# Layer 0's attention heads packed into dense tiles of eight for the output projection, and the projection moved within the order of steps

## The chip, the cores and the metric

The kernel runs on one NeuronCore of a Trainium2 chip. A core has five engines that run side by side: TensorE (PE in the profile; its weight loads are PEld), VectorE (DVE), ScalarE (ACT), GpSimd (POOL) and SyncE (SP, which here only issues transfers). They work on a common on-chip memory, SBUF, of 128 partitions; TensorE writes to a second one, PSUM, whose banks hold 512 float32 values per partition. The metric is the device time of one execution in microseconds (us). A comparison uses the median of several executions.

## The reference, cut to what matters

The model has four layers, each of a cross attention and a feed-forward part, over x of shape (4, 256, 256), four batches of 256 tokens of width 256, with a context of shape (4, 512, 128). All is float32. Only the attention of layer 0 and the step from it to layer 0's feed-forward part are touched:

```python
x = x + _L0_xattn_ref(_layernorm(x), ctx_1024, ...)
x = x + _L0_ffn_ref(_layernorm(x), ...)

def _L0_xattn_ref(x, y, Wq, bq, Wk, bk, Wv, bv, Wkv_dca, bkv_dca, ...):
    # H = 16 heads of HD = 16, DCA = 16
    y_dca, y_main = y[:, -16:, :], y[:, :-16, :]
    kv_dca = (y_dca @ Wkv_dca + bkv_dca).reshape(b, 16, 2, H, HD)
    k_dca, v_dca = _ln(kv_dca[:, :, 0], ...), kv_dca[:, :, 1]
    q = _ln((x @ Wq + bq).reshape(b, s1, H, HD), ...)
    kv = concatenate([y_main @ Wk + bk, y_main @ Wv + bv], -1).reshape(b, s2, H, 2 * HD)
    k, v = _ln(kv[..., :HD], ...), kv[..., HD:]
    ctx = _attn(q, k, v) + _attn(q, k_dca, v_dca)      # both per head, softmax(q k / 4) v
    return ctx @ Wo + bo                               # (256 -> 256)

def _L0_ffn_ref(x, A, B, W, bias):
    vecs = einsum('arh,bsh->bsar', A, x)               # 64 arrows of rank 16
    routes = the four arrows of largest norm, a quarter each
    v = einsum('bsa,bsar->bsr', routes, vecs)
    return x @ W.T + bias + einsum('bsa,ajr,bsr->bsj', routes, B, v)
```

There are thus two softmaxes per head, one over 496 context rows and one over the last 16, and their results are added before the output projection.

## The kernel before

Layer 0's attention (in `bounded_path`, lines 1026 to 1611) stands under a manual schedule: each engine runs its instructions in the order in which the program writes them. What is written first is queued first, and an instruction that waits holds up all behind it on its engine.

The attention loops over the four batches b and, in each, over four groups hg of four heads, each in two steps kp of two context tiles of 128: eight steps i = 2 * hg + kp per batch. A step writes, in this order: `scores` (16 short matmuls into four PSUM banks and four Exp on ScalarE, into pT); `ahead(b, i)` (work for the next batch: the query and key scaling's last product at i = 5, the transposes into qT and kT at 6 and 7); `values` of the group before (matmuls into po) and, where kp is 1, its `quotient`; then `between(b, i)`, the rest of the next batch's preparation (projections at i = 1 to 3, `project_v` among them, the Ln and Exp of the scaling at 4, batch norm statistics at 5 and 6) and `output0` of the batch before. The quotient of a batch's last group is written at i = 1 of the next batch.

Each head has 32 partitions of po: 16 of ones in the values, which give the softmax's denominator, and 16 of the values proper. po has two halves of 256 tokens, for the two softmaxes. `quotient` turns 32x32 blocks of po on VectorE, takes the reciprocal of row 0 of each block, turns it back as a broadcast, multiplies po with it (o), and GpSimd adds the two halves into oT[:, hg]. Half of oT's partitions hold quotients of the ones. `output0` multiplies, per chunk of 128 tokens, the four groups of oT with wo0 (py), whose rows for those partitions are zero (padded on the host); VectorE adds the bias (y_sb) and GpSimd adds that to x_sb. `bias_rows`, `bias_columns` and `output_bias` carry the values' biases through wo0 into bo0.

PSUM banks are handed out by `bank`: while layer 0 runs, all tags but "o" share one ring of six banks in program order, so that a tile waits for the release of the tile six before it; "o" has two of its own. The tag y_sb has two SBUF buffers, shared by output0 and the feed-forward part.

In batch 3 the same places hold layer 0's feed-forward preparation: layer norms (names with f), the `Arrows` of chunk 0 at i = 6 (`vectors`: the matmuls paf and copies into two) and 7 (`routes`: VectorE finds the four largest norms and weighs; GpSimd's last product goes into the second half of two). After the loop (lines 1603 to 1611) come the last values and quotient, the vectors of chunks 1 and 2, the routes of chunk 1, and `output0(B - 1)`; then the pool l0 is closed, and a loop over the eight chunks n runs `routes` of n + 2, `turned` (transposes of two into puT, copied into uT), `vectors` of n + 3 and `output` (pyf, ys, x_sb), with the folding of layer 1's weights between. Those weights' loads (line 969) reuse l0's memory and wait for its last readers.

The call sites of the change, cut:

```python
            if b > 0 and i in (4, 5):
                output0(b - 1, (i - 4,))
...
        for n in (1, 2):
            arrows[n] = Arrows(n)
            arrows[n].vectors()
        arrows[1].routes()
        output0(B - 1)
        c0.close()
```

Of the kernel before, what the change touches and what calls it, by code (L numbers as in the profile page):

```python
# [17 lines left out]
P = 128  # L18
# [817 lines left out]
def bounded_path(ctx: ExitStack, tc: tile.TileContext, t, out: bass.AP, over):  # L836
# [189 lines left out]
    with tc.manual_schedule(engines={E.PE, E.Activation, E.DVE, E.Pool}):  # L1026
# [39 lines left out]
            load_c(b)  # L1066
            load_x(b)

        wo0 = l0.tile([P, 4, D], F32, tag="wo0", name="wo0")
        nc.sync.dma_start(wo0, t["L0_wo"].rearrange("(g p) n -> p g n", p=P))  # L1070
        bo0 = bcast(l0, t["L0_bo"], D, "bo0")
        wa = load_fw("wa", [P, ND, NA * RA], lambda w: [(w, t["F0_aT"].rearrange("(d p) n -> p d n", p=P))], "wa", f0w)
        wb = load_fw("wb", [P, 8, D], lambda w: [(w, t["F0_bT"].rearrange("(k p) n -> p k n", p=P))], "wb", f0w)
# [28 lines left out]

        vals = [l0.tile([P, NK, H0, 32], F32, tag=f"vals{i}", name=f"vals{i}") for i in range(2)]
        vals_d = [l0.tile([P, H0, 32], F32, tag=f"vals_d{i}", name=f"vals_d{i}") for i in range(2)]

        def ones_of_values():
            nc.gpsimd.memset(rows, 1.0)
            nc.gpsimd.affine_select(  # L1110
                out=rows[:, 0:1], in_=rows[:, 0:1], compare_op=ALU.is_ge, fill=0.0, base=RD - 1,
                pattern=[[0, 1]], channel_multiplier=-1,
            )
            nc.gpsimd.affine_select(
                out=rows[:, 1:2], in_=rows[:, 1:2], compare_op=ALU.is_ge, fill=0.0, base=-RD,
                pattern=[[0, 1]], channel_multiplier=1,
            )
            for i in range(2):
                nc.gpsimd.memset(vals[i][:, : NK - 1, :, :HD0], 1.0)
                nc.gpsimd.tensor_copy(  # L1120
                    vals[i][:, NK - 1, :, :HD0], rows[:, 0:1, None].to_broadcast([P, H0, HD0])
                )
                nc.gpsimd.tensor_copy(vals_d[i][:, :, :HD0], rows[:, 1:2, None].to_broadcast([P, H0, HD0]))


        def head_sums(src, p=P):
# [57 lines left out]

        def project_v(b):

            wv = by_head(wkv, 2 * HD0)[:, :, :, HD0:]
            for k0 in range(0, NK + 1, 2):
                pv = bank("mm", [P, 2, H0, HD0], f"pv{b}_{k0}")
                for k in range(k0, min(k0 + 2, NK + 1)):  # L1190
                    ck = c_last[:, b % 2, k - NK + 1, :] if k >= NK - 1 else cT[:, b, k * P : (k + 1) * P]
                    nc.tensor.matmul(pv[:, k - k0], lhsT=ck, rhs=wv[:, int(k == NK)], start=True, stop=True)
                if k0 < NK:
                    nc.scalar.copy(vals[b % 2][:, k0 : k0 + 2, :, HD0:], pv)
                else:
                    nc.scalar.copy(vals_d[b % 2][:, :, HD0:], pv[:, 0])

        class Scale:

# [61 lines left out]
            nc.vector.tensor_tensor(within, wmx[:, 0:1], wmx[:, 1:2], ALU.mult)  # L1261
            nc.vector.tensor_scalar(within, within, SMAX * SMAX * 4.0, None, ALU.is_le)

        bcol = l0.tile([P, 4, P], F32, tag="bcol", name="bcol")

        def bias_rows():

            nc.vector.tensor_tensor(brow[:, 0, :], brow[:, 0, :], brow[:, 1, :], ALU.add)

        def bias_columns():  # L1270
            pc = bank("o", [P, 4], "pbrow")
            for g in range(4):
                nc.tensor.matmul(
                    pc[:, g : g + 1], lhsT=brow[:, 0, g * P : (g + 1) * P], rhs=ident[:1, :1], start=True, stop=True
                )
            nc.vector.tensor_copy(bcol, pc[:, :, None].to_broadcast([P, 4, P]))

        def output_bias():
            pb = bank("mm", [P, D], "pbo")
            for g in range(4):  # L1280
                nc.tensor.matmul(pb, lhsT=bcol[:, g, :], rhs=wo0[:, g, :], start=(g == 0), stop=(g == 3))
            nc.vector.tensor_tensor(bo0, bo0, pb, ALU.add)

        kTs, qTs = {}, {}
# [42 lines left out]
        def values(b, hg, pT, po, ks, dca):  # L1327

            for k in ks:
                for j in range(4):  # L1330
                    nc.tensor.matmul(  # L1331
                        po[32 * j : 32 * (j + 1), 0, :],
                        lhsT=vals[b % 2][:, k, 4 * hg + j, :],
                        rhs=pT[k // 2][:, j, k % 2, :],
                        start=(k == 0),
                        stop=(k == NK - 1),
                    )
            if dca:
                for j in range(4):
                    nc.tensor.matmul(  # L1340
                        po[32 * j : 32 * (j + 1), 1, :],
                        lhsT=vals_d[b % 2][:, 4 * hg + j, :],
                        rhs=pT[1][:, j, 1, :],
                        start=True,
                        stop=True,
                    )

        def quotient(b, hg, po, oT):

            NB0 = 2 * S // 32  # L1350
            po = po.rearrange("p a s -> p (a s)")
            z = w0.tile([P, NB0, 32], F32, tag="z0", name=f"z0_{b}_{hg}")
            z_f = z.rearrange("p f i -> p (f i)")
            nc.vector.transpose(z_f, po)
            rz = small.tile([P, NB0], F32, tag="rz0", name=f"rz0_{b}_{hg}")
            nc.vector.reciprocal(rz, z[:, :, 0])
            nc.vector.transpose(z, rz[:, :, None].to_broadcast([P, NB0, 32]))
            o = w0.tile([P, 2, S], F32, tag="o0", name=f"o0_{b}_{hg}")
            nc.vector.tensor_tensor(o.rearrange("p a s -> p (a s)"), po, z_f, ALU.mult)
            nc.gpsimd.tensor_tensor(oT[:, hg, :], o[:, 0], o[:, 1], ALU.add)  # L1360

        def output0(b, chunks=range(NC)):
            for c in chunks:
                py = bank("mm", [P, D], f"py0_{b}_{c}")
                for hg in range(4):
                    nc.tensor.matmul(
                        py,
                        lhsT=oTs[b][:, hg, c * P : (c + 1) * P],
                        rhs=wo0[:, hg, :],
                        start=(hg == 0),  # L1370
                        stop=(hg == 3),
                    )
                y_sb = w0.tile([P, D], F32, tag="y_sb", name=f"y_sb{b}_{c}")
                nc.vector.tensor_tensor(y_sb, py, bo0, ALU.add)
                nc.gpsimd.tensor_tensor(x_sb[b][:, c, :], x_sb[b][:, c, :], y_sb, ALU.add)
# [83 lines left out]
        xn = norm.tokens()  # L1459
        warm(8)  # L1460
        xnTs[0] = layernorm_T(xn, "a0_0")
        centred(by_head(wq0), by_head(wq0), mq)
        centred(by_head(crow), by_head(crow), head_sums(by_head(crow), 3), 3)
        wk = by_head(wkv, 2 * HD0)[:, :, :, :HD0]
# [48 lines left out]
        def between(b, i):  # L1513

            n = b + 1
            if n < B:
# [21 lines left out]
                    norms[n + 1] = Norm(n + 1, f"a0_{n + 1}")  # L1538
                elif i == 6 and n + 1 < B:
                    xns[n + 1] = norms[n + 1].tokens()  # L1540
            if b > 0 and i in (4, 5):
                output0(b - 1, (i - 4,))
            if b == 0:
                if i == 0:
                    bias_rows()
# [38 lines left out]

        before = None
        for b in range(B):
            oTs[b] = w0.tile([P, 4, S], F32, tag="oT0", name=f"oT0_{b}")
            for hg in range(4):
                pT = [
                    w0.tile([P, 4, 2, S], F32, tag="pT0", name=f"pT0_{b}_{hg}_{kp}", bufs=3) for kp in range(2)  # L1590
                ]
                for kp in range(2):
                    scores(b, hg, pT, kp)
                    ahead(b, 2 * hg + kp)
                    if before:
                        if kp == 0:
                            po = bank("o", [P, 2, S], f"po0_{b}_{hg}")
                        values(*before, po, (2 * kp, 2 * kp + 1), kp == 1)
                        if kp == 1:
                            quotient(*before[:2], po, oTs[before[0]])  # L1600
                    between(b, 2 * hg + kp)
                before = (b, hg, pT)
# [3 lines left out]
        for n in (1, 2):  # L1606
            arrows[n] = Arrows(n)
            arrows[n].vectors()
        arrows[1].routes()
        output0(B - 1)  # L1610
        c0.close()

# [13 lines left out]
        for n in range(B * NC):  # L1626
            if n + 2 < B * NC and n != 5:
                arrows[n + 2].routes()
            if c2s:
                b, c2 = c2s.pop()  # L1630
                nc.vector.tensor_reduce(csq[:, b * NK : (b + 1) * NK], c2, AX.X, ALU.add)
            arrows[n].turned()
            if n % NC == 0:
                if n + 3 < B * NC:
                    arrows[n + 3] = Arrows(n + 3)
                    arrows[n + 3].vectors()
                for _ in range((0, 0, 1, 1, 2, 2, 1, 1)[n]):
                    next(fold)
                arrows[n].output()
            else:  # L1640
                arrows[n].output()
                k = n // NC + 2
                if k < B:
                    xnTs["f", k] = layernorm_T(xns["f", k + (k == 2)], f"f0_{k}")
                for _ in range((0, 0, 1, 1, 2, 2, 1, 1)[n]):
                    next(fold)
                if n == 5:
                    arrows[7].routes()
                if n + 3 < B * NC:
                    arrows[n + 3] = Arrows(n + 3)  # L1650
                    arrows[n + 3].vectors()
# [1545 lines left out]
```

## Time and profile before

| | us |
|---|---|
| median of 3 runs (lowest to highest) | 1463.46 (1458.37 to 1465.62) |
| the profiled execution's own time | 1460.66 |
| its span, first to last instruction | 1458.9 |
| mean granted TensorE clock | 0.992 |
| TensorE busy in the span | 1422.8 |
| layer 0's attention, first scores to last py | 25.1 to 172 |

The profile shows one execution. Busy time of TensorE is the time in which a matmul is in flight; the duration of a row of the profile is from issue to end and contains the pipeline's latency, so that the price of a matmul in a stream is better read from the distance of two starts. A wait is put down to the releaser that came last by the profile. The chain that ended last follows the work back from the last instruction and tells which engine's instruction set the pace at each time.

### The profile page before, as it was taken

To read this page: it belongs to the slowest core of one execution; us is meant where nothing else is said; L and a number is where in the kernel's file an instruction comes from. 1 tells how busy PE (TensorE), PEld (TensorE's weight loads), DVE (VectorE), ACT (ScalarE), POOL (GpSimd) and SP (SyncE) were. 2 spreads that over 40 slices of the span, in tenths; PEclk is the share of its full clock that TensorE was granted. 3 is DMA by queue.
4 is the path that set the end of the run, shared out by engine and by line. 5 is a ranking of instruction groups with operands and counts; after the bars stand their busy time and mean duration, and the time that the engine had idled before them with its cause. 6 is when DMAs were issued, how large, how long until landed. Compare 5 with 4: busy or idle time off the path is not lost.

```text
span 1458.9 us, 20220 instructions
## 1 busy us (share of the span) xinstructions
PE 1422.8 (98%) x7421; PEld 937.1 (64%) x7421; DVE 912.8 (63%) x2004; ACT 585.9 (40%) x1124; POOL 678.8 (47%) x796
## 2 busy tenths in 40 slices
PE   8999999999999999999999999999999999999997
PEld 7666567565566666877555666656875566666656
DVE  5666783566766557543577566557755766767675
ACT  4666443433433332244543333333454433333331
POOL 3122232486545455132356665655313765456560
PEclk9999999999999999999999999999999999999999
DMA  5000111310000000264120000000241000000000
GB/s 166 2 1 2 48 61 37 74 36 0 8 1 8 1 0 9 62 189 119 33 66 8 19 4 1 8 1 8 86 132 44 19 1 1 0 1 0 0 1 32
DMA packets 49591, 47.06 MB, mean 32 GB/s; under 512 B 8169, under 2 KB 45386, under 8 KB 49484
## 3 DMA queue, kind: packets, MB, share of 16 engines
q1 hardware_dynamic: 45884, 37.56, 8.6%
q0 software_dynamic: 2496, 6.82, 1.8%
q8 instruction: 61, 1.00, 0.3%
q10 hardware_dynamic: 1104, 1.31, 0.3%
q14 instruction: 46, 0.38, 0.1%
HBM read 38.86 MB, written 6.82 MB: 31 GB/s over the span
## 4 chain that ended last, share of the span: by engine, by line
PE 88%; DVE 7%; POOL 2%; issue 1%; ACT 1%; DVEq 0%; ACTq 0%; POOLq 0%
PE ps L1818 22%; PE po L1826 21%; PE paq L1788 5%; PE pao L1788 4%; PE pbq L1788 4%; PE pbo L1788 4%; PE pgu L2326 2%; PE ps L1321 2%; PE po L1331 2%; PE pyf L1448 2%; PE paf L1398 1%; PE py L1908 1%; PE pm L985 1%; PE psh L2162 1%; PE pn L1001 1%
## 5 line engine op out<-in xcount | busy, mean ns | idle before, releaser
L1837 POOL TENSOR_TENSOR half<-pT 128x1024 f32<-128x1024 f32 x93 | 218.8, 2353 | 320.7 <-ACT pT L1821 262.4
L1818 PE MATMUL ps<-qT,cT 128*128 128x512 f32 x768 | 345.5, 592 | 0.0
L1826 PE MATMUL po<-pT,c_sb 128*128 128x512 f32 x768 | 345.3, 592 | 0.0
L1821 ACT ACTIVATE pT<-ps,mbias 128x512 f32<-128x512 f32 x384 | 263.7, 687 | 155.5 <-PE ps L1818 142.2
L1826 PEld LDWEIGHTS po<-pT,c_sb 128*128 128x128 f32 x768 | 145.8, 190 | 183.2 <-issue 183.2
L1818 PEld LDWEIGHTS ps<-qT,cT 128*128 128x128 f32 x768 | 138.9, 190 | 138.4 <-issue 137.0
L1830 ACT COPY oT<-po 128x512 f32<-128x512 f32 x96 | 56.2, 586 | 265.0 <-PE po L1826 265.0
L1873 POOL TENSOR_TENSOR oT<-oT,wide 128x512 f32<-128x512 f32 x90 | 115.5, 1302 | 28.1 <-DVE wide L1872 28.1
L1325 ACT ACTIVATE pT<-ps 128x512 f32<-128x512 f32 x128 | 66.1, 603 | 42.0 <-PE ps L1321 41.8
L1798 DVE TENSOR_TENSOR qT<-qT,paq 128x128 f32<-128x128 f32 x90 | 25.4, 282 | 85.9 <-ACT qT L1797 85.8
L1798 DVE TENSOR_TENSOR w<-w,pao 128x128 f32<-128x128 f32 x21 | 6.0, 285 | 109.3 <-ACT w L1797 109.3
L1847 DVE STREAM_TRANSPOSE turned<-half 128x512 f32<-128x512 f32 x96 | 68.3, 711 | 6.3
L1845 DVE TENSOR_TENSOR half<-half 128x512 f32<-128x512 f32 x96 | 70.6, 735 | 2.5 <-POOL half L1837 2.2
L1788 PEld LDWEIGHTS paq<-xnT_a,m_sb 128*128 128x128 f32 x360 | 57.9, 191 | 21.5 <-issue 10.6
L1788 PE MATMUL paq<-xnT_a,m_sb 128*128 128x128 f32 x360 | 71.4, 280 | 0.1
L1788 PE MATMUL paq<-xx,m_x 128*128 128x128 f32 x360 | 69.8, 275 | 0.0
L1851 DVE TENSOR_REDUCE sums<-turned 128x16 f32<-128x512 f32 x96 | 65.8, 686 | 3.3
L1788 PE MATMUL pao<-n_x,ox 128*128 128x128 f32 x336 | 65.2, 276 | 0.3 <-POOL ox L1714 0.3
L1872 DVE STREAM_TRANSPOSE wide<-rz 128x512 f32<-128x512 f32 x96 | 62.2, 685 | 0.1
L1797 ACT COPY qT<-paq 128x128 f32<-128x128 f32 x90 | 23.9, 265 | 88.7 <-PE paq L1788 88.7
L1801 DVE TENSOR_TENSOR qT<-qT,pbq 128x384 f32<-128x384 f32 x90 | 49.8, 554 | 9.4
L1788 PEld LDWEIGHTS paq<-xx,m_x 128*128 128x128 f32 x360 | 54.7, 192 | 0.0
(445 smaller groups left out, 2614.6 us busy)
## 6 DMA issues: line engine op xcount, KB each, us to landing
wo<-in_L_wo SPq DMA_DIRECT2D x12, 512.0 KB
wq<-in_L_wqT SPq DMA_DIRECT2D x11, 512.0 KB
yd<-yr SPq DMA_DIRECT2D x23, 128.0 KB
w<-in_F_w SPq DMA_DIRECT2D x4, 512.0 KB
xd<-xn_f SPq DMA_DIRECT2D x7, 256.0 KB
wk<-in_L_wkT SPq DMA_DIRECT2D x11, 128.0 KB
wv<-in_L_wvT SPq DMA_DIRECT2D x11, 128.0 KB
x_sb<-in_x SPq DMA_DIRECT2D x4, 256.0 KB
```

The lines of the kernel that those rows point to most:

```text
L1325: nc.scalar.activation(pT[kp][:, j], ps[j], AF.Exp)
L1788: nc.tensor.matmul(p[:, at, :], lhsT=lhsT, rhs=rhs, start=(k == 0 and at == 0), stop=(k == len(of) - 1 and i == which[-1]),)
L1818: nc.tensor.matmul(ps, lhsT=cT[:, b, k * P : (k + 1) * P], rhs=qT, start=True, stop=True)
L1821: nc.scalar.activation(pT[:, k, :], ps, AF.Exp, bias=mbias[:, b, k : k + 1])
L1826: nc.tensor.matmul(po, lhsT=c_sb[:, b, k, :], rhs=pT[:, k], start=(k == 0), stop=(k == NK - 1))
L1830: done["head"] = nc.scalar.copy(raw, po).ins
L1837: nc.gpsimd.tensor_tensor(half, pT[:, 0:2], pT[:, 2:4], ALU.add)
L1845: nc.vector.tensor_tensor(part, half[:, 0], half[:, 1], ALU.add)
L1847: nc.vector.transpose(turned.rearrange("p f i -> p (f i)"), part)
L1851: nc.vector.tensor_reduce(sums[b, hp // 4][:, hp % 4, :], turned, AX.X, ALU.add)
L1872: nc.vector.transpose(wide, rzs[b, hp // 4][:, hp % 4, :, None].to_broadcast([P, NB, 32]))
L1873: eng.tensor_tensor(outs[b, hp], outs[b, hp], wide.rearrange("p f i -> p (f i)"), ALU.mult)
```

## The change

The values of four heads and their ones are stored in two ways: for even groups hg the ones stand in the first 16 of a head's 32 partitions, for odd groups in the last 16. The reciprocal is turned back with zeros for the ones' partitions (rz0, two tiles set to zero once, of which every quotient writes one column), so that the product o is zero there. An even group and the odd one after it are then added into one tile of oT of eight heads: two halves for the even group (one GpSimd addition), and two more for the odd one (two additions). oT and wo0 have two tiles instead of four, output0 two matmuls per chunk instead of four, and the bias functions are cut alike. wo0 is loaded by eight transfers of 16 partitions, which pick its rows. The value weights are first copied by GpSimd into wvo, in the order of the new tiles, and project_v evicts each bank in two copies. ones_of_values follows.

In the order of work, output0 of the batch before goes from steps 4 and 5 to steps 6 and 7, except in batch 3, and after the loop `turned` and `output` of chunk 0 stand before output0 of batch 3 instead of in the loop over n.

```diff
-        wo0 = l0.tile([P, 4, D], F32, tag="wo0", name="wo0")
-        nc.sync.dma_start(wo0, t["L0_wo"].rearrange("(g p) n -> p g n", p=P))
+        wo0 = l0.tile([P, 2, D], F32, tag="wo0", name="wo0")
+        wo0r = t["L0_wo"].rearrange("(q o j i x) n -> o j i x q n", q=2, o=2, j=4, i=2)
+        for o in range(2):
+            for j in range(4):
+                r0 = 32 * j + HD0 * (1 - o)
+                nc.sync.dma_start(wo0[r0 : r0 + HD0], wo0r[o, j, 1])
...
+        halves = [(slice(HD0, 32), slice(0, HD0)), (slice(0, HD0), slice(HD0, 32))]
+        rz0 = [l0.tile([P, 2 * S // 32, 2], F32, tag=f"rzh{i}", name=f"rzh{i}") for i in range(2)]
+        wvo = l0.tile([P, 2, 2, H0 // 2, HD0], F32, tag="wvo", name="wvo")
...
                 for k in range(k0, min(k0 + 2, NK + 1)):
...
-                    nc.tensor.matmul(pv[:, k - k0], lhsT=ck, rhs=wv[:, int(k == NK)], start=True, stop=True)
-                if k0 < NK:
-                    nc.scalar.copy(vals[b % 2][:, k0 : k0 + 2, :, HD0:], pv)
-                else:
-                    nc.scalar.copy(vals_d[b % 2][:, :, HD0:], pv[:, 0])
+                    nc.tensor.matmul(pv[:, k - k0], lhsT=ck, rhs=wvo[:, int(k == NK)], start=True, stop=True)
+                for o, (h, _) in enumerate(halves):
+                    if k0 < NK:
+                        nc.scalar.copy(vals[b % 2][:, k0 : k0 + 2, o, :, h], pv[:, :, o])
+                    else:
+                        nc.scalar.copy(vals_d[b % 2][:, o, :, h], pv[:, 0, o])
...
         def output_bias():
             pb = bank("mm", [P, D], "pbo")
-            for g in range(4):
-                nc.tensor.matmul(pb, lhsT=bcol[:, g, :], rhs=wo0[:, g, :], start=(g == 0), stop=(g == 3))
+            for g in range(2):
+                nc.tensor.matmul(pb, lhsT=bcol[:, g, :], rhs=wo0[:, g, :], start=(g == 0), stop=(g == 1))
...
             nc.vector.transpose(z_f, po)
-            rz = small.tile([P, NB0], F32, tag="rz0", name=f"rz0_{b}_{hg}")
-            nc.vector.reciprocal(rz, z[:, :, 0])
-            nc.vector.transpose(z, rz[:, :, None].to_broadcast([P, NB0, 32]))
+            odd = hg % 2
+            rz = rz0[odd]
+            nc.vector.reciprocal(rz[:, :, 1 - odd], z[:, :, HD0 * odd])
+            nc.vector.transpose(
+                z.rearrange("p f (i x) -> p f i x", i=2), rz[:, :, :, None].to_broadcast([P, NB0, 2, HD0])
+            )
             o = w0.tile([P, 2, S], F32, tag="o0", name=f"o0_{b}_{hg}")
             nc.vector.tensor_tensor(o.rearrange("p a s -> p (a s)"), po, z_f, ALU.mult)
-            nc.gpsimd.tensor_tensor(oT[:, hg, :], o[:, 0], o[:, 1], ALU.add)
+            oT = oT[:, hg // 2, :]
+            nc.gpsimd.tensor_tensor(oT, oT if odd else o[:, 1], o[:, 0], ALU.add)
+            if odd:
+                nc.gpsimd.tensor_tensor(oT, oT, o[:, 1], ALU.add)
 
         def output0(b, chunks=range(NC)):
             for c in chunks:
                 py = bank("mm", [P, D], f"py0_{b}_{c}")
-                for hg in range(4):
+                for q in range(2):
                     nc.tensor.matmul(
                         py,
-                        lhsT=oTs[b][:, hg, c * P : (c + 1) * P],
-                        rhs=wo0[:, hg, :],
...
+                        lhsT=oTs[b][:, q, c * P : (c + 1) * P],
+                        rhs=wo0[:, q, :],
...
         xnTs[0] = layernorm_T(xn, "a0_0")
+        for n in range(2):
+            wv = by_head(wkv, 2 * HD0)[:, n, :, HD0:].rearrange("p (q o j) x -> p o q j x", q=2, o=2)
+            for o in range(2):
+                nc.gpsimd.tensor_copy(wvo[:, n, o].rearrange("p (q j) x -> p q j x", q=2), wv[:, o])
...
-            if b > 0 and i in (4, 5):
-                output0(b - 1, (i - 4,))
+
+            i0 = 4 if b == B - 1 else 6
+            if b > 0 and i in (i0, i0 + 1):
+                output0(b - 1, (i - i0,))
...
         arrows[1].routes()
+        arrows[0].turned()
+        arrows[0].output()
         output0(B - 1)
         c0.close()
...
-            arrows[n].turned()
+            if n:
+                arrows[n].turned()
             if n % NC == 0:
...
-                arrows[n].output()
+                if n:
+                    arrows[n].output()
```

## The prediction

> **What bounds the kernel.** I read the page first, then the rows of the lines that the edit touches, then the chain that ended last between 58 and 182 us, and last the timeline around each wait in it.
>
> ```profile
> span 1458.9 us, 20220 instructions
> PE 1422.8 (98%) x7421; PEld 937.1 (64%) x7421; DVE 912.8 (63%) x2004; ACT 585.9 (40%) x1124; POOL 678.8 (47%) x796
> PE 88%; DVE 7%; POOL 2%; issue 1%; ACT 1%; DVEq 0%; ACTq 0%; POOLq 0%
> ```
>
> TensorE is the bound: a matmul taken away counts in full, unless TensorE then meets a wait. Layer 0's attention runs from about 25 to 172 us.
>
> ```profile
> L1366 PE MATMUL py<-wo,oT x64: 379/379/483, 78.4 to 171.8; 128*128 128x256 f32 x64
> L1360 POOL TENSOR_TENSOR oT<-o x16: 722/728/825, 46.0 to 169.0; 128x256 f32<-128x256 f32 x16
> ```
>
> Each float32 matmul stands as two records, so output0's 32 matmuls are 64, eight per chunk. The 379 ns are latency; the price is the pitch, in the chain (start, duration in us, what):
>
> ```profile
> 78.49 1.94 PE py L1366 x8
> 80.45 0.42 DVE y_sb L1374
> ...
> 82.12 1.76 DVE pad L1231
> ...
> 87.55 0.34 DVE y_sb L1374
> 87.93 1.09 PE pT L1296 x8
> ...
> 120.89 0.34 DVE y_sb L1374
> 121.28 1.09 PE pT L1296 x8
> ...
> 134.82 1.06 DVE xn_f L925 x2
> ...
> 169.01 0.73 POOL oT L1360
> 169.79 2.43 PE py L1366 x10
> ```
>
> A chunk costs 1.94 us. In batches 1 and 2 the chain leaves TensorE between 80 and 88 and at 120: step 6's transposes take a PSUM bank of the ring of six that step 5's py holds until VectorE, behind pad and a quotient, has added the bias. The timeline (start, duration, instruction, in brackets the idle time before and its releaser) gives the waits:
>
> ```profile
> 87.93 0.85 PEld L1296 LDWEIGHTS pT<-ident,pad 128*128 128x128 f32 x8 [1.66 <-DVE y_sb L1374]
> 134.90 0.82 POOL L1360 TENSOR_TENSOR oT<-o 128x256 f32<-128x256 f32 x1 [2.87 <-DVE o L1359]
> 166.69 1.93 POOL L1427 TENSOR_TENSOR twof<-routef,vf 128x1024 f32<-128x1024 f32 x1 [5.65 <-DVE vf L1426]
> 169.78 2.02 PEld L1366 LDWEIGHTS py<-wo,oT 128*128 128x128 f32 x10 [1.99 <-POOL oT L1360]
> ```
>
> **The change part by part, for the profiled execution** (1460.66 us, span 1458.9; 1.8 us lie outside the span, and the shown runs' median is 2.8 us higher, so I take the difference to the median).
>
> *Start.* project_v's evictions go from three to six on ScalarE. Rows: 128x512 copies 585 ns, 128x256 378 ns, and a 128x128 copy elsewhere (L1797) 265 ns. Back to back the three start at 16.81, about 17.3 and 17.75 and make way at 18.02, 1.21 us; four at about 0.28 and two at about 0.17 are 1.46. Behind them wait the Ln of the query scale (18.02), its pad, and TensorE's transposes (20.13), with 0.06 us to spare: **+0.2**. For batches 1 to 3 ScalarE idles 0.28 to 0.69 us around these copies. wvo's four POOL copies fit between 7.67, where POOL goes idle, and 14.05, where project_v starts: a 128x112 copy is 0.28 to 0.57 us, and one copy blocked by VectorE took 0.89, so 1.2 to 3.6 us. Uncovered they would cost that. ones_of_values grows by some 0.7 us of POOL near 22; its consumers start at 37.4. The eight wo0 issues on SP at about 0.45 us push bo0, wa, wb, ww, bias0 and the mask 3.2 us back; first use of wo0 is at 45.4, of the mask 61.8, of wa 151: nothing.
>
> *Bias.* bias_columns loses 4 of 8 records; seven took 0.87 us at 35.55, on TensorE's path: **-0.45**. output_bias loses half of its 1.94 us, but TensorE then waits anyway: from 43.43 the chain is on VectorE without a gap (z, hv, he, pad) until the transposes at 52.04. **0**; it would be -0.97 if that chain were shorter.
>
> *Batch 1, steps 4 to 7.* Scores of step 5 start at 78.5, not 80.43. hr comes off ScalarE at 80.11 as before, since it stands behind step 4's Exps. VectorE's he need no longer wait behind y_sb (80.45), and its second product takes 0.26 us, not the 0.72 it took beside POOL's x_sb addition: pad ends at 82.76, not 83.88. TensorE is there at 82.2, waits 0.65, transposes (1.46), values 1.00, py at half price 0.97: step 7 at 86.3, not 90.02. Now the ring: with py inside step 6, step 7's fourth score bank is that of the second transpose, which VectorE evicts only after pad, the quotient and the batch norm statistics (82.76 + 2.5 + 1.37 + 0.81), 87.5. Scores end at 88.2, not 91.1. Transposes wait 0.1 for y_sb; transposes, values and the rest 2.9, py 0.97: the next batch starts at 92.2, not 93.99. **-1.8.**
>
> *Batch 2.* The same count: pad at 117.4, transposes until 118.9, values, py, step 7 at 120.9 (the bank is free at 120.7, there being no next norm), next batch 125.84, not 127.36. **-1.5.** The waits removed here and in batch 1 are partly replaced by those for pad and the bank.
>
> *Batch 3.* Its two chunks stay in steps 4 and 5, 0.97 us less each: **-1.94**. Odd quotients put a second addition of 0.73 us on POOL, eight in all. Behind it stand oT's reader (late steps, over 10 us away) and VectorE operations that POOL blocks. The row: xn_f at 134.74 takes 820 ns beside POOL's addition, 404 alone, and TensorE waits for it at 135.26 and 135.93. This quotient is odd, so a second addition follows directly: 0 to 0.75, **+0.35** taken, half-way, because the blocked VectorE operation may get in between the two. The rule that speaks against the change is in the Trainium skill (GPSIMD Engine Reference, Specifications): POOL's SBUF interfaces are shared with VectorE and contend with its two-port modes and with two SBUF inputs. Were all eight additions to block the path, the rule gives 8 x 0.73 = 5.8 us, an estimate. The rows limit it: after the other odd quotients follow y_sb or qk (PSUM and one SBUF input; L1168 beside a POOL addition takes its usual 0.68), statistics or nothing.
>
> *End.* Before: paf until 166.74, six py records, wait until 169.79, ten more, turned, paf of chunk 3, output until 180.84. After: turned(0) waits for POOL's twof at 168.62, so the wait of about 2 us stays and only changes its cause. Then turned 0.87, output 0.86 + 3.45 (uT is copied during the first), py 8 records at 0.213 = 1.7, paf 3.44: 179.02. oT, now two additions after twof, is ready at 170.5 and needed at 173.9. **-1.8.** What is late next: the second y_sb shares two buffers with ys, freed by POOL only behind twof of chunk 1 (176.4) and its own addition, at 177.1; VectorE's routes(2) starts 2.7 us later. Their product was ready at 182.8 and is read at 190.25 by TensorE, now 1.8 earlier: 2.9 us remain. The raw loads behind c0.close waited for y_sb (175.09), are needed at 194.99, and move by under 2 us. At 232 to 241 TensorE waits again on VectorE, whose chain there starts from TensorE's own pn, so the gain passes through.
>
> Sum: 0.2 - 0.45 - 1.8 - 1.5 - 1.94 + 0.35 - 1.8 = **-6.95 us**; 1463.46 - 7 = **1456.5**.
>
> **Rivals.** (a) *Larger gain*: the bank wait in step 7 (1.0 with y_sb's) doesn't come, and batch 3's cold stretch goes. The clock row:
>
> ```profile
> 138.00:140.00 2.00, 2.00 (x24) 0.77 (x20) 0.07 (x1) 1.59 (x4) 0.00 (x0) 0.50 0.00 0
> ```
>
> (the last three columns are granted clock, DMA share and GB/s.) Half clock from 137.8 to 141.8 cost 0.58 + 0.42 + 0.62 = 1.6 us. Then -7 - 1.0 - 1.6 = -9.6, 1453.9. For it: a cold stretch hangs on where TensorE's idle time falls, and every start shifts. Against: the xn_f wait stays. (b) *Part is absorbed*: the routing chain on VectorE at 160 to 176 is as long as TensorE's work; if VectorE's 2.7 us are not covered and the start loses more, 4 us go: -3, 1460.5. For it: TensorE waits there already. Against: 2.9 us of slack. (c) *Slower*: new half-clock stretches. They cost 1.6 us at 138 and 0.94 + 1.69 = 2.6 at 30 to 35, 2.1 on average. From four of them (new waits in steps 6 and 7 of batches 1 and 2, and the end) the gain is gone: -7 + 4 x 2.1 = +1.4, 1464.9. The Trainium skill (TensorE: Matmul & The Clock Gate, Part 1) has the clock fall after an idle window of some 3.4 us; by that rule waits of 0.65 to 2 us cost nothing and (c) is nil. The trace is harsher: 1.2 and 0.2 us of idle inside 134 to 136 were enough. But waits of 1.4 at 86.5 and 1.6 at 168.2 left the clock at 1.00, so a stretch per wait is the exception, and four are unlikely. (d) *The moves do nothing*: the halved records alone give 8 x 0.97 + 0.45 - 0.55 = -7.7, 1455.8; nearly the same time, told apart by the waits alone.
>
> **How the numbers follow.** Forecast with (d) 0.55, own range 1454.5 to 1458.5 (half a us for each of four estimated terms); (a) 0.25; (b) 0.15; (c) 0.05. The runs before spread by 0.5%, 7.3 us, which is about what a measurement can tell from no change. The range 1451 to 1461.5 takes in (a) and (b) with the runs' scatter and leaves (c) out. Faster by over 0.5%, below 1456.1: (a) and a bit under half of the forecast, 0.50. Slower by over 0.5%: less than half of (c), 0.02. Within: 0.48.
>
> **What would show it.** py has 32 records, each chunk 0.97 us in the chain. The wait for y_sb at step 6 is gone; in its place waits for pad of under 1 us and, in batch 1 alone, for the fourth bank. xn_f's wait in batch 3 is up to 0.75 longer. turned(0) waits about 2 us for twof, and no py waits for oT. Half clock shows twice, near 30 and 135. The stages after 250 us keep their lengths. I am wrong if the end's waits grow beyond 2.5 us, if project_v's first matmul waits for wvo, or if a third cold stretch shows.

## The result, and the profile after

The changed kernel takes 1454.80 us (median; 1452.88 to 1461.86), the kernel before, run beside it, 1463.19 us (1458.16 to 1469.85). The ratio of the compared runs is 0.9962, with a 95% interval of 0.9948 to 0.9976: 5.6 us less, where 7 were forecast. The runs of both kernels scatter over some 10 us, because TensorE's clock falls in the first 50 us of some executions and not of others (two traces of the changed kernel below differ by 6.8 us in span, 6.5 of them there); so the medians differ by 8.4 us, and the ratio, with its interval, is what I go by.

The head of the changed kernel's page, and the two rows that answer to those shown of before:

```profile
span 1459.7 us, 20196 instructions
PE 1423.3 (98%) x7381; PEld 936.3 (64%) x7381; DVE 913.0 (63%) x2005; ACT 586.2 (40%) x1136; POOL 686.1 (47%) x816
PE 88%; DVE 6%; POOL 2%; issue 1%; ACT 1%; DVEq 0%; ACTq 0%; POOLq 0%
...
L1392 PE MATMUL py<-wo,oT x32: 379/379/483, 92.8 to 178.6; 128*128 128x256 f32 x32
...
L1386 POOL TENSOR_TENSOR oT<-oT,o x8: 722/725/731, 62.3 to 173.1; 128x256 f32<-128x256 f32 x8
```

py has 32 records instead of 64, and POOL has eight second additions. But the span is 0.8 us longer than before's, and TensorE's busy time has not fallen. The windows near the start say why (start to end, length, busy time of PE, PEld, DVE, ACT, POOL with counts, granted clock, DMA share, GB/s):

```profile
18.00:20.00 2.00, 0.58 (x4) 0.58 (x5) 1.80 (x6) 1.94 (x10) 0.00 (x0) 0.94 0.82 240
20.00:22.00 2.00, 2.00 (x10) 1.98 (x11) 0.89 (x4) 0.33 (x1) 1.53 (x8) 0.50 1.01 393
```

In this execution TensorE waited 1.68 us, until 19.42, and its matmuls then ran at half clock. That isn't the change: another execution of the same kernel waited 1.69 us at the same place, kept its clock there, and had a span of 1453.0. The timeline, of this execution and of the other:

```profile
19.42 2.44 PE L1254 MATMUL pcols<-ident,rep 1*128 1x1 f32 x12 [1.68 <-DVE rep L1511]
```

```profile
19.24 1.49 PE L1254 MATMUL pcols<-ident,rep 1*128 1x1 f32 x12 [1.69 <-DVE rep L1511]
```

And a kernel with the start of before (the order alone, below) lost it there too. So no two spans may be subtracted here; stages have to be. I cut the traces at the same instructions in each kernel (lengths in us; of the changed kernel, the execution without the early stretch; the last two columns are the pair of both kernels with filler matmuls, of which more below):

| stage | before | after | before, filled | after, filled |
|---|---|---|---|---|
| first project_v to first scores | 10.80 | 10.90 | 10.80 | 10.90 |
| batch 0, steps 0 to 3 | 18.24 | 17.91 | 15.18 | 14.73 |
| batch 0, steps 4 to 7 | 15.95 | 16.38 | 15.96 | 16.37 |
| batch 1, steps 0 to 3 | 17.09 | 17.09 | 17.09 | 17.09 |
| batch 1, steps 4 to 7 | 17.58 | 16.31 | 17.58 | 16.30 |
| batch 2, steps 0 to 3 | 17.05 | 17.05 | 17.05 | 17.05 |
| batch 2, steps 4 to 7 | 16.32 | 15.10 | 16.33 | 15.10 |
| batch 3, steps 0 to 3 | 12.52 | 12.98 | 11.52 | 11.52 |
| batch 3, from step 4 to the quotient in step 7 | 17.85 | 16.02 | 17.22 | 16.02 |
| from there to `turned` of chunk 1 | 23.01 | 21.41 | 23.00 | 21.41 |
| from there to layer 1's first query matmul | 69.73 | 69.92 | 69.73 | 69.91 |
| the rest | 1208.45 | 1207.11 | 1206.85 | 1208.09 |

From the first project_v to `turned` of chunk 1, the changed kernel is 5.26 us shorter, in the filled pair 5.24. (The unfilled pair can be compared because both executions lost the clock at the same two places, near 30 and near 136 us.) Right behind it 0.18 us are lost again: in every kernel with the new end, chunk 1's uT is copied later, since ScalarE has the copies of paf before it. The rest varies by some 2 us from one execution to the next of kernels that are the same there. The chain of waits of the changed kernel (start, duration, what):

```profile
93.70 0.58 DVE ve_a L919
94.28 0.72 DVE qT L1327
95.05 1.13 PE ps L1340 x10
...
99.07 1.06 PE py L1392 x4
...
169.89 1.93 POOL twof L1453
171.87 1.09 PE puTf L1461 x8
...
177.28 1.73 PE py L1392 x8
```

py costs 1.06 us a chunk instead of 1.94, and no y_sb stands in batches 1 and 2 any more. At the end TensorE waits for twof, and py follows without a wait for oT. ve_a, one VectorE instruction on 128x2 values, takes 0.58 us here. It stood in the chain of before too, in the same two batches, at 0.17:

```profile
55.42 0.17 DVE ve_a L919
...
87.38 0.17 DVE ve_a L919
```

The timeline round these places, of the changed kernel:

```profile
90.35 1.50 PE L1315 MATMUL pT<-ident,pad 128*128 128x128 f32 x12 [0.59 <-DVE pad L1244]
...
93.54 0.72 POOL L1386 TENSOR_TENSOR oT<-oT,o 128x256 f32<-128x256 f32 x1
93.70 0.58 DVE L919 TENSOR_SCALAR ve_a<-mv_a 128x2 f32<-128x2 f32 x1
95.05 1.13 PE L1340 MATMUL ps<-qT,kT 16*128 16x256 f32 x10 [0.50 <-DVE qT L1327]
...
171.87 1.09 PE L1461 MATMUL puTf<-ident,twof 128*128 128x128 f32 x8 [1.76 <-POOL twof L1453]
...
180.26 0.42 DVE L1400 TENSOR_TENSOR y_sb<-py,bo 128x256 f32<-128x256 f32 x1 [1.66 <-POOL x_sb L1477]
```

The waits are those that the prediction put in place of the old ones: 0.59 us for pad, 0.50 for step 7's fourth bank, 1.76 for twof, and VectorE's 1.66 for the second y_sb, which no later matmul waits for.

### The profile page after: what moved, and what is told of

The parts are those of the page before. It is cut to its first block, busy times and chain, and to the rows that moved or that the text cites. A ratio compares the mean times of both kernels' runs of the same rounds, so it can differ in the third digit from the quotient of the medians.

```text
span 1459.7 us, 20196 instructions
## 1 busy us (share of the span) xinstructions
PE 1423.3 (98%) x7381; PEld 936.3 (64%) x7381; DVE 913.0 (63%) x2005; ACT 586.2 (40%) x1136; POOL 686.1 (47%) x816
## 4 chain that ended last, share of the span: by engine, by line
PE 88%; DVE 6%; POOL 2%; issue 1%; ACT 1%; DVEq 0%; ACTq 0%; POOLq 0%
PE ps L1854 22%; PE po L1862 21%; PE paq L1824 5%; PE pao L1824 4%; PE pbq L1824 4%; PE pbo L1824 4%; PE pgu L2362 2%; PE ps L1340 2%; PE pyf L1474 2%; PE po L1350 2%; PE paf L1424 1%; PE py L1944 1%; PE psh L2198 1%; PE pm L985 1%; PE pn L1001 1%
```

## The experiments

**The two halves of the change.** First the changed kernel again, beside the dense tiles in the old order and the new order with four tiles. Dense tiles alone, against the changed kernel:

```diff
-            i0 = 4 if b == B - 1 else 6
+            i0 = 4
...
         arrows[1].routes()
-        arrows[0].turned()
-        arrows[0].output()
         output0(B - 1)
...
-            if n:
-                arrows[n].turned()
+            arrows[n].turned()
```

(`output` in the loop likewise.) The new order alone is the same edit the other way round, made to the kernel before.

> The changed kernel again, as the mark for the other three. Theory (the sum of its parts, all in layer 0's attention): 5 to 6 us under the kernel before. Rival (the difference of two medians is mostly luck of the TensorE clock): under 3 us. In its profile py has 32 records, step 6's transposes wait under 1 us in batch 1, turned(0) waits about 2 us for twof, and VectorE's ve_a takes 0.58 us in step 5 of batches 0 and 1 instead of 0.17, because the second addition on GpSimd stands beside it.

> The dense tiles alone; the order of before in all places (output0 in steps 4 and 5, chunk 0's arrows after the last projection). Theory: py at 1.06 us instead of 1.94 counts in full only in batch 3 (-1.8); in batch 1 VectorE's chain (y_sb, pad, quotient, ve_a, y_sb) stays and gives -0.3, in batch 2 -0.7, the bias -0.4, batch 0 +0.4 through ve_a, and at the end the wait for oT grows by the second addition and takes the matmuls saved: -0.1. About -2.9 in all, so some 2.7 us slower than the changed kernel. Rival (the moves do nothing): the same time as the changed kernel within 1 us.

> The moves alone, with the four tiles of before. Theory: the waits removed at steps 4 to 6 are replaced by the wait for pad, for the bank of the second transpose and at the end for twof; batches 1 and 2 together 0 to +0.6, the end +0.1: within 1 us of the kernel before. Rival (the moves bring the gain): 2 to 3 us faster than before.

Measured, with the kernel before at 1462.12 us: the changed kernel 1456.25, ratio 0.9968 (0.9950 to 0.9986), 4.7 us by the ratio and 5.9 by the medians; dense tiles alone 1462.55, ratio 1.0015 (1.0000 to 1.0030); the order alone 1462.55, ratio 1.0005 (0.9988 to 1.0023). The dense tiles alone bring nothing. That misses my expectation of -2.9 us: I had the saved matmuls turning into waits, but not what the waits do to the clock. Timeline and windows of the kernel with dense tiles alone, at step 6 of batch 1:

```profile
95.45 1.11 PE L1315 MATMUL pT<-ident,pad 128*128 128x128 f32 x4 [2.26 <-DVE y_sb L1400]
96.50 1.94 PE L1350 MATMUL po<-pT,vals 128*32 128x256 f32 x16
```

```profile
94.00:96.00 2.00, 0.55 (x3) 0.55 (x4) 1.93 (x5) 0.62 (x1) 1.82 (x4) 0.82 0.00 0
96.00:98.00 2.00, 2.00 (x19) 0.76 (x17) 1.66 (x7) 0.78 (x1) 0.55 (x1) 0.50 0.00 0
```

The transposes wait 2.26 us for the bank that y_sb frees, and behind that wait the clock is 0.50: 16 records of the values take 1.94 us, at full clock 1.07. Steps 4 to 7 take 18.45 us in batch 1 and 17.35 in batch 2, where before they took 17.58 and 16.32 with twice the py work. The order alone gains 0.75 us in batch 1, loses 0.51 in batch 2, and gives nothing in all, as expected; its trace has no half clock in these batches or at the end. (At the start it has: from the first project_v to the first scores it took 14.10 us.) So neither half carries the gain: the dense tiles need the new order, which gives TensorE the freed time as work.

**The end alone put back.** The changed kernel, with `turned` and `output` of chunk 0 behind output0 of batch 3 again (the part of the diff above that follows the first "...").

> The changed kernel with only the end put back: output0 of batch 3 before turned and output of chunk 0. Theory: TensorE then waits for oT until both additions are done, some 3 us instead of 1.8, and works off six py records behind it: 1.2 us slower than the changed kernel, from z of step 7 to turned of chunk 1 22.8 us instead of 21.6. Rival: no difference, since the wait is there either way.

Measured: 1457.71 us, ratio 0.9980 (0.9965 to 0.9994). The end takes 24.47 us against 21.41, 3.06 more, where I had 1.2. The timeline, and the windows at the same place:

```profile
166.31 2.93 PE L1392 MATMUL py<-wo,oT 128*128 128x256 f32 x6 [3.31 <-POOL oT L1386]
```

```profile
164.00:166.00 2.00, 0.00 (x0) 0.00 (x0) 1.96 (x4) 0.00 (x0) 1.46 (x3) 0.97 0.00 0
166.00:168.00 2.00, 1.69 (x4) 1.41 (x5) 1.76 (x5) 0.00 (x0) 0.26 (x1) 0.50 0.00 0
```

py now waits 3.31 us for oT, whose two additions stand behind twof on POOL, and again half clock follows. Two causes are mixed here, the wait and the clock. To part them, 12 filler matmuls (`warm`, which the kernel uses at its start: products of the identity into a bank that nobody reads) go into the wait:

```diff
+        warm(12)
         output0(B - 1)
         c0.close()
```

> The changed kernel with the end in the old order, as in the run with only the end put back (end 24.47 us against 21.41), and 12 filler matmuls of 128x128 written ahead of output0 of batch 3, where TensorE waits 3.31 us for oT. Theory: the excess over the wait itself is the clock, which falls in that wait: with the fillers the matmuls of py and turned behind it run at full clock, py's six records fall from 2.93 to about 1.3 us, and the end takes 22.7 to 23.1 us. Rival: the second POOL addition and the order alone set the end, and it stays at 24.3 to 24.6; the fillers themselves may even cost up to 0.5.

```profile
169.27 2.84 PE L1407 MATMUL pwarm<-ident 128*128 128x128 f32 x24
171.95 0.60 PE L1392 MATMUL py<-wo,oT 128*128 128x256 f32 x2
173.19 1.56 PE L1392 MATMUL py<-wo,oT 128*128 128x256 f32 x6 [0.64 <-POOL oT L1386]
```

The end falls from 24.47 to 23.02 us, within what the theory gave, and the six records from 2.93 to 1.56, where it had 1.3. 23.02 is also what the end took before (23.01): in the old order, even at full clock, the halved py gains nothing there. Of the 3.06 us, 1.45 are the clock and 1.61 the wait. The whole time, 1458.89 us (ratio 0.9973, 0.9957 to 0.9989), can't show 1.45 us: its runs reach from 1453.12 to 1464.86.

**The second addition beside VectorE.** In the changed kernel the second POOL addition of an odd group runs while VectorE computes the next norm's ve_a, on the way to qT and the scores' bank. Written behind the step's other work, it comes after that norm's instructions:

```diff
-            if odd:
-                nc.gpsimd.tensor_tensor(oT, oT, o[:, 1], ALU.add)
+            return lambda: odd and nc.gpsimd.tensor_tensor(oT, oT, o[:, 1], ALU.add)
...
-                            quotient(*before[:2], po, oTs[before[0]])
+                            rest = quotient(*before[:2], po, oTs[before[0]])
                     between(b, 2 * hg + kp)
+                    if before and kp == 1:
+                        rest()
...
-        quotient(*before[:2], po, oTs[B - 1])
+        quotient(*before[:2], po, oTs[B - 1])()
```

> The changed kernel with the second addition of odd groups written after the step's other work, so that on GpSimd rstd comes first and VectorE's ve_a is not beside an addition. Theory: ve_a in step 5 of batches 0 and 1 is back to about 0.17 us, and each of the two batches, whose chain runs through it, is 0.4 us shorter: 0.8 us faster than the changed kernel. Rival (as the prediction had it, the additions meet only xn_f in batch 3): no difference in batches 0 and 1, up to 0.4 in batch 3.

```profile
93.77 0.17 DVE L919 TENSOR_SCALAR ve_a<-mv_a 128x2 f32<-128x2 f32 x1
94.01 0.70 POOL L920 TENSOR_TENSOR rstd_a<-ve_a,neghalf 128x2 f32<-128x2 f32 x1 [0.49 <-DVE ve_a L919]
94.68 0.72 POOL L1385 TENSOR_TENSOR oT<-oT,o 128x256 f32<-128x256 f32 x1
```

ve_a takes 0.17 us instead of 0.58. In the changed kernel it ended when the addition did (above: 93.70 + 0.58 = 94.28, and 93.54 + 0.72 = 94.26), so it was held up and not only slowed. Steps 4 to 7 of batch 0 take 15.96 us instead of 16.38, those of batch 1 15.95 instead of 16.30: -0.77, as expected. The time is 1453.15 us, ratio 0.9957 (0.9937 to 0.9976); its interval and that of the changed kernel overlap.

**The clock at the start.** To take the scatter out, both kernels got fillers at the three places where TensorE's idle time had been followed by half clock: ahead of `norm_columns`, of batch 1's first norm transposes, and of those of f0 in batch 3. (The third kernel has the late addition too.)

```diff
         context_T(1)
+        warm(7)
         norm_columns()
...
                         xns[1] = norms[1].tokens()
+                        warm(10)
...
                     k = i // 2 - 1
+                    if k == 0:
+                        warm(4)
```

> The kernel before with idle TensorE time filled by matmuls whose result nobody reads, in three places: 7 before norm_columns, 10 before the transposes of batch 1's first norm, 4 before those of f0 in batch 3. Theory of the clock: the half-clock stretches near 30 to 35 us and 138 to 142 us go, and the runs that are 4 to 10 us longer than the shortest with them: the lowest run 2 to 4 us under the lowest of before, the median 5 to 7, the spread under 2 us. Rival (the spread comes from transfers or elsewhere): the spread stays at 8 us and more and the median moves by under 2 us.

> The changed kernel with the same three fillings. Theory: as for the kernel before, and against it the same 5 to 6 us that the parts give, now with both at full clock. Rival (part of the change's gain is its luck with the clock): the two filled kernels differ by under 4 us.

> The changed kernel with the fillings and the late second addition. Theory: the two effects add, 0.8 us under the filled changed kernel, and some 10 us under the median of the kernel before. Rival: no more than the fillings alone.

Measured beside the kernel before at 1461.47 us:

| | us | lowest to highest | ratio, 95% interval |
|---|---|---|---|
| before, filled | 1456.27 | 1454.26 to 1458.53 | 0.9961 (0.9949 to 0.9973) |
| after, filled | 1450.83 | 1449.92 to 1451.32 | 0.9929 (0.9906 to 0.9952) |
| after, filled, late addition | 1448.48 | 1448.00 to 1450.67 | 0.9916 (0.9893 to 0.9939) |

The kernel before scatters over 4.3 us instead of 11.3; I had expected under 2. The same windows as above, of the filled changed kernel:

```profile
18.00:20.00 2.00, 1.88 (x17) 1.69 (x17) 1.83 (x5) 1.94 (x11) 0.00 (x0) 1.00 0.83 216
20.00:22.00 2.00, 1.94 (x19) 1.88 (x19) 1.71 (x8) 0.69 (x2) 1.41 (x7) 1.00 0.97 380
```

Steps 0 to 3 of batch 0 fall from 17.91 to 14.73 us, and the runs lie within 1.4 us of each other. (A group of fillers also takes a bank of the ring; the stages without fillers keep their lengths within 0.02 us.) Between the two filled kernels the change is worth 1456.27 - 1450.83 = 5.44 us, and their runs don't overlap. That agrees with their stages (5.24), but only within the scatter of the rest. The last kernel is faster than both, by 13 us against before. Its late addition shows 0.75 us in the stages; the remaining 1.6 of its 2.35 us lie in the rest of the program. There the two traces part at one place, some 360 us behind layer 1's first query matmul: half clock lasts 6.83 us there in the filled changed kernel and 3.41 in the one with the late addition. In the filled kernel before, which has no such addition, it lasts 3.41 too; so I don't count that as the addition's.

**Dense tiles alone with a warm start**, so that their failure is not due to the start: the first edit with the fillers.

> The dense tiles with the old order everywhere, with the 7 + 10 + 4 filler matmuls that also went into the kernel before (1456.27) and the changed one (1450.83), so that the start and the stretch at 135 us keep their clock. No filler stands in batch 1's and batch 2's step 6 or at the end, where the old order makes TensorE wait. Theory: batches 1 and 2 stay at 18.45 and 17.35 us, the end at 24.5, and the time is that of the filled kernel before within 1.5 us (1456 to 1458.5), so that the dense tiles without the moves bring nothing even with a warm start. Rival: the dense tiles bring part of their 7.7 us once the start is undisturbed (1450 to 1454).

It takes 1457.91 us, ratio 0.9971 (0.9959 to 0.9983), beside 0.9961 for the filled kernel before: no gain. Its timeline, steps 6 of batch 1 and of batch 2:

```profile
85.59 0.66 PE L1315 MATMUL pT<-ident,pad 128*128 128x128 f32 x4 [2.26 <-DVE y_sb L1400]
86.18 1.07 PE L1350 MATMUL po<-pT,vals 128*32 128x256 f32 x16
...
117.94 1.83 PE L1315 MATMUL pT<-ident,pad 128*128 128x128 f32 x8 [1.30 <-DVE y_sb L1400]
119.70 1.94 PE L1350 MATMUL po<-pT,vals 128*32 128x256 f32 x16
```

Here my expectation of 18.45 us for batch 1 missed: the same wait of 2.26 us left the clock alone this time (why, the last section tells), and the stage took 16.99, 0.59 less than before. The wait of 1.30 us in batch 2 brought it down, and 17.34 came out, 1.01 more. So the dense tiles in the old order save about a third of their 1.74 us in a batch (0.59) where the clock stays, and lose more where it falls. Fillers in those steps weren't tried: the transposes wait there for a bank, and a filler would take one from the same ring.

## Why the prediction was right or wrong

By its own steps, measured on the filled pair, in which no half clock of the start or of batch 3 disturbs:

| step | predicted | measured |
|---|---|---|
| start | +0.2 | +0.10 |
| bias_columns, output_bias | -0.45, 0 | -0.45 |
| batch 0, steps 4 to 7 | 0 | +0.41 |
| batch 1 | -1.8 | -1.28 |
| batch 2 | -1.5 | -1.23 |
| batch 3, with xn_f | -1.94 + 0.35 | -1.20 |
| end | -1.8 | -1.59 |
| sum | -6.94 | -5.24 |

**Right**: the start and the bias, each within 0.1; the places and causes of the new waits in step 6 of batch 1 (0.65 us forecast for pad, 0.59 measured) and at the end (about 2 us for twof, 1.76); the ring's fourth bank as the wait of step 7; and VectorE's later y_sb, covered by the slack. project_v's first matmul did not wait for wvo. That the moves are needed the prediction left open: it gave its forecast and rival (d) one chance together, since both came to some 7 us. And the measured 1454.80, within its own range and even under its 1456.5, is in part luck: the change gave 1.4 us less than forecast, and the median of the same kernel was 1456.25 in the next series.

The sum is 1.7 us too large, for the three reasons that follow, 0.2 us at the end and 0.1 in batch 2 that I didn't trace.

*The price of a chunk.* I halved 1.94 us to 0.97; it takes 1.06. The chain's piece has a part that doesn't halve. A chunk saves 0.87 to 0.88, so that 0.18 is missing in each of three batches, 0.5 in all.

*The second addition.* The prediction looked for operations that POOL blocks and listed, after the odd quotients other than batch 3's, "y_sb or qk", "statistics or nothing". The step that failed is "statistics": behind the batch norm statistics follows ve_a, a VectorE instruction of 0.17 us that becomes 0.58 beside the addition, twice, in batches 0 and 1, and qT and the scores' bank stand behind it. Its sum for step 7 had ve_a in it (the 1.37 us of statistics), at the 0.17 of before. That is 0.77 of the 1.7 us, and the late addition gives it back. The rule from the Trainium skill (GPSIMD Engine Reference, Specifications) had named the shared interfaces; the error was to look only at large instructions.

*xn_f in batch 3.* The prediction took +0.35; it cost 0.53, at another place and for another cause. At step 2, where I put it, nothing changed. The changed kernel's timeline:

```profile
139.67 1.14 DVE L925 TENSOR_SCALAR xn_f<-x_sb,mv_f,rstd_f 128x256 f32<-128x256 f32 x2
139.89 0.76 POOL L1384 TENSOR_TENSOR oT<-oT,o 128x256 f32<-128x256 f32 x1 [3.66 <-DVE o L1381]
...
140.73 0.72 POOL L1386 TENSOR_TENSOR oT<-oT,o 128x256 f32<-128x256 f32 x1
140.86 0.20 PEld L937 LDWEIGHTS pxn_f<-ident,xn_f 128*128 128x128 f32 x2 [0.47 <-DVE xn_f L925]
```

The pair of xn_f takes 1.14 us, as in the filled kernel before: its second instruction ends at 140.80, 0.15 us behind the first addition and 0.65 ahead of the end of the second. The loss came two steps later, at step 4, where py had covered xn_f. The timelines of the filled kernel before and of the filled changed kernel:

```profile
138.20 1.99 PE L1366 MATMUL py<-wo,oT 128*128 128x256 f32 x8
140.03 0.60 PE L937 MATMUL pxn_f<-ident,xn_f 128*128 128x128 f32 x4
140.56 1.15 PE L1321 MATMUL ps<-qT,kT 16*128 16x256 f32 x16
```

```profile
136.24 1.13 PE L1392 MATMUL py<-wo,oT 128*128 128x256 f32 x4
137.25 0.41 PE L937 MATMUL pxn_f<-ident,xn_f 128*128 128x128 f32 x2
137.89 0.44 PE L937 MATMUL pxn_f<-ident,xn_f 128*128 128x128 f32 x2 [0.24 <-DVE xn_f L925]
138.26 1.15 PE L1340 MATMUL ps<-qT,kT 16*128 16x256 f32 x16
```

From py to the next scores it was 2.36 us and is 2.02: 0.34 of the 0.87 saved arrive, the rest is waiting for the second xn_f. That wait belongs to the shorter py, not to a second addition: none stands near it, and the late addition leaves this stage at 16.02 us. So "0.97 us less each" is the step that hid it.

**The rivals.** The larger gain (a) didn't come: the bank wait in step 7 stayed, and half clock in batch 3 showed in both traces of the changed kernel (it comes and goes: in those with the late addition or the old end it didn't). Absorption (b), -3 us, named the wrong place; its mechanism acted at ve_a and xn_f instead of the end. (c), new half-clock stretches, does not describe the change but one half of it: with the dense tiles in the old order there is a stretch in each of batches 1 and 2 and one at the end, and with the waits ahead of them they took away what these tiles save there; the new order alone has none of them. I gave it a few per cent by looking at the new waits only; for the changed kernel, whose new waits are under 1.8 us and left the clock alone in every trace of it, that was right. It can fall there, though: in the kernel with the old end, which is the same up to that place, half clock followed the wait for pad in step 6 of batch 0 (1.48 us there; before, TensorE idled 1.12), and steps 4 to 7 took 16.75 us instead of 16.38. Rival (d), "the moves do nothing", falls: it put the halved records alone at -7.7 us, and they measured +2.2, with an interval from 0 to +4.4. The text's "half clock shows twice, near 30 and 135" holds for some executions only; in the profiled one it shows at 20 to 26 too. That is the third cold stretch by which the prediction would have called itself wrong, but it was a poor sign: the kernel with the start of before has it as well.

## What to carry to other kernels

Work taken from the bounding engine is worth what the order lets it use: give the saved time something to do in the same step, or it becomes a wait. When an engine gets a new instruction, look at the smallest instructions beside it too, if they stand on the path. Where runs scatter, cut the traces into stages between fixed instructions and fill the idle spots that let the clock fall, before believing a difference of spans.

## What was not expected of the hardware

Waits far shorter than the 3.4 us that the Trainium skill gives for an idle window (TensorE: Matmul & The Clock Gate, Part 1) brought the clock to half: 1.30, 1.68 and 2.26 us. And one wait had two outcomes: 1.68 us at 19.42 lost the clock and 1.69 us in another execution of the same kernel kept it; 2.26 us lost it in one trace and kept it in another; those of 1.42 and 1.76 us kept it. The page also says that the window runs freely, and the traces agree: in all twelve, each stretch from one recorded change of the granted clock to the next is a whole multiple of 3.41 us (3.41, 6.83, 13.65, 23.89, 102.4). So it matters where in these windows a wait falls. The two waits of 2.26 us, cut by them; first the dense tiles alone, then the same with a warm start:

```profile
91.87:95.29 3.42, 1.25 (x9) 0.77 (x8) 3.25 (x9) 2.73 (x5) 1.58 (x3) 1.00 0.02 5
95.29:98.70 3.41, 3.25 (x24) 1.65 (x28) 2.37 (x8) 0.78 (x1) 1.26 (x2) 0.50 0.00 0
```

```profile
80.58:83.99 3.41, 2.68 (x26) 1.56 (x24) 3.27 (x8) 1.96 (x5) 0.32 (x1) 1.00 0.00 0
83.99:87.41 3.42, 1.81 (x24) 1.06 (x28) 3.35 (x9) 1.55 (x3) 2.52 (x4) 1.00 0.00 0
87.41:90.82 3.41, 3.41 (x48) 2.46 (x48) 2.19 (x7) 2.47 (x5) 0.00 (x0) 1.00 0.00 0
```

In the first, 2.10 of the 2.26 us lie in one window, TensorE is busy for 1.25 us of it, and the next window runs at half clock. In the second the wait is shared between two windows, and the clock stays. In the twelve traces, each of the 27 windows at full clock with less than 1.4 us of busy TensorE was followed by half clock. But a threshold is not shown: of two windows with the wait of 1.68 us, one with 1.74 us busy lost the clock and one with 1.73 kept it, and even one with 3.15 us, at 593 us in the filled changed kernel, was followed by half clock.

A fall cost 1 to 1.6 us in a batch (0.4 in batch 0's steps 4 to 7), and some 3 in steps 0 to 3 of batch 0 (18.24 against 15.18). Fillers of 7, 10 and 4 matmuls, placed in idle time, took 5.2 us off the kernel before (1461.47 to 1456.27), about as much as the whole change.
